# Cross-attention on one core: each square's first key block in two column parts

## The chip, the cores and the metric

The kernel runs on one core of a Trainium2 chip. The metric is the device time of one execution in microseconds, lower is better; for the kernel before it is the median of three runs.

## What is computed

Two batches of 2048 tokens with 640 channels attend, in 20 heads of 32 channels, to 77 text tokens and to 77 image tokens. Both have a softmax of their own, and the two results are added before the output projection.

```python
q = _split_heads(hidden_states @ Wq.T, H)
k = _split_heads(text @ Wk.T, H)
v = _split_heads(text @ Wv.T, H)
out_text = _merge_heads(_attend(q, k, v, sm_scale))
k_ip = _split_heads(ip @ Wk_ip.T, H)
v_ip = _split_heads(ip @ Wv_ip.T, H)
out_ip = _merge_heads(_attend(q, k_ip, v_ip, sm_scale))
out = out_text + IP_SCALE * out_ip
out = out @ Wo.T + bo
return out + residual
```

Everything is float32.

## The kernel before

The channels are cut in `NC` = 5 chunks of 128, that is four heads (`G` = 4) of 32 channels. A pair `q` is one chunk of one batch; there are 10 pairs. A unit `u` is half a pair's tokens (1024); there are 20. For each unit the kernel makes the queries (`queries`, line 201, in full 128x128 matmuls of 512 columns), the scores of each token against the 154 keys (`scores`, line 233), and the two softmaxes in the tensor `pb`, with the maximum, the exponential, the sum and the division shared among the vector, scalar and GpSimd engines (DVE, ACT, POOL). A 32x32 transpose on DVE (`transpose`, line 323) then turns the probabilities so that the keys lie on the partitions. The 154 keys fill `NK` = 5 blocks of 32 (the last has 26 and is filled up with zeros).

When both units of a pair are transposed, `attend` (line 332) multiplies with the values. The tensor engine is used as 16 tiles of 32x32, called squares here and numbered in the order of the code: row group `r` is the tile's rows and its PSUM bank (`pa[r]`), column group `g` the head and the 32 partitions of that bank. A matmul of one square and one key block `k` has 512 columns: 16 runs of 32 tokens each, in the layout that the transpose leaves. The loop goes block by block over all 16 squares, so a square's five blocks are accumulated in its own quarter of a bank. `v4s[q % 2]` holds the values, spread over the row groups by DMAs; `take_attention` (lines 355 and 359, on ACT) copies the four banks out, the first bank first.

The order of all work is written out by hand: each word of `SCHEDULE` emits one step on its engines. `A.q` is an attend, `CA.q` its copies out, `R` are scores, `q` queries, `m` and `F` the products of the output projection (lines 490, 500 and 848), `o` its last chunk (line 471), `k` and `v` the projections of keys and values (line 142). The 8 PSUM banks are two halves of four; the number behind an `@` names the half or the bank. The ten attends stand between queries or scores ahead of them and scores, queries or products behind them.

A float32 matmul is shown in the profile as two passes, each with its weight load: the 800 matmuls of line 332 are 1600 passes and 1600 loads.

Of the kernel before, what the change touches and what calls it, by code (L numbers as in the profile page):

```python
# [15 lines left out]
H, D, TEXT = 20, 32, 77  # L16
# [4 lines left out]
def kernel(  # L21
# [25 lines left out]
    nc = tc.nc  # L47
# [3 lines left out]
    G = P // D  # L51
# [9 lines left out]
    NK = (2 * L + D - 1) // D  # L61
# [28 lines left out]
    v4s = [const.tile([P, G, NK, D], F32, name=f"v4_{n}") for n in range(2)]  # L90
# [234 lines left out]
    def attend(q, pa):  # L325

        zones = pb[:, ds(q % 2, SUB)].rearrange("p z n g (k s) -> p (z n) g k s", k=NK)
        for k in range(NK):
            for r in range(G):
                rows = slice(r * D, (r + 1) * D)  # L330
                for g in range(G):
                    nc.tensor.matmul(  # L332
                        pa[r][g * D : (g + 1) * D, :],
                        v4s[q % 2][rows, g, k, :],
                        zones[rows, :, g, k, :],
                        start=(k == 0),
                        stop=(k == NK - 1),
                    )

    def rows_of_attention(b, c):  # L340

# [290 lines left out]
    def emit(word):  # L632
# [7 lines left out]
        elif k == "A":  # L640
            at[name] = halves[int(where)]
            attend(x, at[name])
        elif k == "CA":
            take_attention(x, at[f"A.{x}"])
# [246 lines left out]
```

## Time and profile before

| | |
|---|---|
| median of the runs | 497.76 us (497.68 to 497.79, 3 runs) |
| span of the profiled execution | 496.7 us |
| around the span, against the median | 1.06 us |
| TensorE busy with matmuls | 490.3 us (99%), 4114 passes |
| DVE, ACT, POOL busy | 408.5, 315.0, 362.5 us |
| line 332, the attends | 55.2 us in 10 pieces, 1600 passes |
| granted TensorE clock | full, in all 40 slices |

The profile is of one execution and gives its span, from the first to the last instruction; that execution's whole time isn't given apart from it, so the table sets the span beside the median. PE is the tensor engine's matmuls, PEld its weight loads. The listed durations of passes that follow one another overlap, so a busy PE isn't one at its peak. The chain that ended last is followed back from the last instruction, at each step to what released it.

### The profile page before, as it was taken

The page shows a single profiled execution, that of the slowest core. Times are in us where ns is not written, and L with a number is a line of the kernel's source. Part 1 is how long each engine was busy: PE and PEld are TensorE (multiplying, and loading weights), DVE is VectorE, ACT ScalarE, POOL GpSimd, SP SyncE. Part 2 cuts the span into 40 slices and gives each one's busy share as a digit, 9 for nine tenths or more (in the row PEclk, how much of TensorE's full clock was granted, in tenths as well). Part 3 has the DMA queues.
Part 4 walks back from the last instruction along what each step waited for, and adds up shares of the span by engine and source line. Part 5 has one row for each costly group of instructions (what it writes and reads, how often), then busy time and mean ns, then how long its engine had stood idle before and what let it go on. Part 6 is the DMA issues. An engine that isn't in the chain of part 4 may idle for free.

```text
span 496.7 us, 10482 instructions
## 1 busy us (share of the span) xinstructions
PE 490.3 (99%) x4114; PEld 287.9 (58%) x4114; DVE 408.5 (82%) x412; ACT 315.0 (63%) x1021; POOL 362.5 (73%) x157
## 2 busy tenths in 40 slices
PE   8999999999999999999999999999999999999997
PEld 5676657657547556456647654755755675444442
DVE  0069989979979989969976896687999978898877
ACT  1165878978978778668999786587578966100000
POOL 0069978798888999989874858565899888284830
PEclk9999999999999999999999999999999999999999
DMA  8991440332360454886445177418525401420115
GB/s 259 356 246 40 132 120 1 106 93 69 92 213 3 132 178 132 274 273 237 158 152 191 58 244 210 133 57 246 174 69 171 127 23 43 149 84 1 43 73 223
DMA packets 67474, 69.38 MB, mean 140 GB/s; under 512 B 5473, under 2 KB 47201, under 8 KB 67425
## 3 DMA queue, kind: packets, MB, share of 16 engines
q1 hardware_dynamic: 66704, 68.00, 43.8%
q8 instruction: 32, 0.52, 0.5%
q10 hardware_dynamic: 720, 0.72, 0.4%
q14 instruction: 18, 0.14, 0.1%
HBM read 54.94 MB, written 10.49 MB: 132 GB/s over the span
## 4 chain that ended last, share of the span: by engine, by line
PE 92%; DMA 3%; SPq 1%; DVE 1%; POOL 1%; ACT 1%; issue 0%; POOLq 0%
PE bank L201 33%; PE bank L848 11%; PE bank L490 10%; PE bank L233 10%; PE bank L332 10%; PE bank L142 9%; PE bank L471 6%; PE bank L500 3%; DMA aT<-in_L_xattn_Wk_ip_dram 2%; DMA wq<-in_L_xattn_Wq_dram 2%; SPq L534 1%; POOL pb L316 1%; DVE den L306 0%; ACT pb L301 0%; SPq L132 0%
## 5 line engine op out<-in xcount | busy, mean ns | idle before, releaser
L316 POOL TENSOR_TENSOR pb<-pb,rden 128x1848 f32<-128x1848 f32 (+1 forms) x60 | 176.1, 2944 | 39.7 <-DVE rden L311 35.5
L201 PE MATMUL bank<-x,wq 128*128 128x512 f32 x400 | 180.4, 601 | 0.6 <-DMA x<-in_x_dram 0.5
L295 POOL TENSOR_TENSOR pb<-pb,mx 128x1848 f32<-128x1848 f32 (+1 forms) x38 | 119.3, 3152 | 51.8 <-DVE mx L281 51.5
L201 PEld LDWEIGHTS bank<-x,wq 128*128 128x128 f32 x400 | 74.1, 191 | 86.7 <-issue 80.8
L323 DVE STREAM_TRANSPOSE pb<-pb 128x1920 f32<-128x1920 f32 (+1 forms) x60 | 115.7, 1932 | 4.9 <-POOL pb L316 4.3
L281 DVE TENSOR_REDUCE mx<-pb 128x24 f32<-128x1848 f32 (+1 forms) x51 | 93.7, 1850 | 30.7 <-ACT pb L245 30.5
L245 ACT COPY pb<-bank 128x462 f32<-128x462 f32 (+1 forms) x204 | 87.2, 539 | 36.0 <-PE bank L233 35.4
L306 DVE TENSOR_REDUCE den<-pb 128x24 f32<-128x1848 f32 (+1 forms) x47 | 88.7, 1895 | 17.6 <-ACT pb L301 13.3
L301 ACT ACTIVATE pb<-pb 128x1848 f32<-128x1848 f32 (+1 forms) x38 | 64.2, 1696 | 17.8 <-POOL pb L295 17.5
L269 ACT ACTIVATE pb<-pb,mx 128x77 f32<-128x77 f32 x224 | 67.8, 364 | 0.3 <-DVE mx L281 0.2
L233 PEld LDWEIGHTS bank<-kT,qT 32*128 32x128 f32 x1280 | 45.4, 184 | 26.9 <-issue 15.6
L269 ACT ACTIVATE pb<-bank,mx 128x77 f32<-128x77 f32 x184 | 51.8, 386 | 9.3 <-DVE mx L284 9.3
L233 PE MATMUL bank<-kT,qT 32*128 32x154 f32 x1280 | 56.2, 305 | 0.3 <-ACT kT L559 0.3
L332 PE MATMUL bank<-pb,v 32*32 32x512 f32 x1600 | 55.2, 597 | 0.0
L142 PE MATMUL bank<-wo_ct,aT 128*128 128x154 f32 x320 | 45.6, 296 | 0.3 <-DMA aT<-in_L_xattn_Wk_ip_dram 0.3
L142 PEld LDWEIGHTS bank<-wo_ct,aT 128*128 128x128 f32 x320 | 42.9, 188 | 3.6 <-issue 2.2
L332 PEld LDWEIGHTS bank<-pb,v 32*32 32x32 f32 x1600 | 29.9, 103 | 22.8 <-issue 10.7
L211 ACT ACTIVATE qT<-bank 128x512 f32<-128x512 f32 x40 | 24.2, 619 | 22.1 <-PE bank L201 22.0
L471 PE MATMUL bank<-aT,wo_ct 128*128 128x512 f32 x80 | 36.1, 596 | 0.0
L269 ACT ACTIVATION_READ_ACCUMULATOR pb<-bank,mx 128x1 f32 x128 | 33.6, 267 | 0.0
L490 PE MATMUL bank<-aT,wo_ct 128*128 128x256 f32 x128 | 32.3, 385 | 0.0
L490 PEld LDWEIGHTS bank<-aT,wo_ct 128*128 128x128 f32 x128 | 23.7, 190 | 6.5 <-issue 3.0
(75 smaller groups left out, 434.4 us busy)
## 6 DMA issues: line engine op xcount, KB each, us to landing
x<-in_x_dram SPq DMA_DIRECT2D x20, 1280.0 KB, 6.7
out_dram<-acc SPq DMA_DIRECT2D x20, 256.0 KB, 2.3
x<-in_x_dram SPq DMA_DIRECT2D x18, 256.0 KB, 5.9
acc<-in_x_dram SPq DMA_DIRECT2D x16, 256.0 KB, 4.7
out_dram<-x SPq DMA_DIRECT2D x15, 256.0 KB, 2.0
v<-vS SPq DMA_DIRECT2D x160, 20.0 KB, 2.8
wq<-in_L_xattn_Wq_dram SPq DMA_DIRECT2D x9, 320.0 KB, 5.0
aT<-in_L_xattn_Wk_dram SPq DMA_DIRECT2D x5, 512.0 KB, 5.5
```

Of the source, the lines that this page charges most:

```text
L142: nc.tensor.matmul(keys_in(out), loaded[n][:, k, :], cT[:, k, :, t, :], start=(k == 0), stop=(k == NCC - 1))
L201: nc.tensor.matmul(pq, wqs[q % 3][:, k, :], xs[place_of(u, h)][:, k, :], start=(k == 0), stop=(k == NC - 1),)
L233: nc.tensor.matmul(ps[g][:, ts(t, 2 * L)], qTs[(u, h)][g * D : (g + 1) * D, ts(st, P)], kT[g * D : (g + 1) * D, c, b].rearrange("p t l -> ...
L245: nc.scalar.copy(keys_of(u, s)[:, :, g], ps[g][:, : n * 2 * L].rearrange("p (n l) -> p n l", n=n))
L269: nc.scalar.activation(row, row if ps is None else rows_in(ps[g], n)[:, t, x], AF.Exp, bias=maxs[(u, s)][:, *one], accum_out=None if den i ...
L281: nc.vector.tensor_reduce(mx, rows_of(u, s), AX.X, ALU.max, negate=negate)
L295: nc.gpsimd.tensor_tensor(rows_of(u, s), rows_of(u, s), maxs[(u, s)].unsqueeze(3).to_broadcast([P, n, 2, L]), ALU.subtract)
L306: nc.vector.tensor_reduce(den_of(u, s), rows_of(u, s), AX.X, ALU.add)
L316: nc.gpsimd.tensor_tensor(rows_of(u, s), rows_of(u, s), rdens[(u, s)].unsqueeze(3).to_broadcast([P, n, 2, L]), ALU.mult)
L323: nc.vector.transpose(p, p)
L332: nc.tensor.matmul(pa[r][g * D : (g + 1) * D, :], v4s[q % 2][rows, g, k, :], zones[rows, :, g, k, :], start=(k == 0), stop=(k == NK - 1),)
L490: nc.tensor.matmul(part, w_of[m][:, kp, op], t_of(m, b, i)[:, kp], start=(op == kp == 0 and m in (1, 2, 5)), stop=(op == 1 and kp == 1 and ...
```

## The change

`attend` alone is changed. For key block 0, the 32 columns of each of the 16 runs are cut in two: square `i` (0 to 15) first does the first `12 + i` of 32, which starts the accumulation. Then the blocks 1 to 4 follow whole, over all squares in the same order. At the end, square `i` does the remaining `20 - i` columns of block 0, and that matmul ends the accumulation. An attend has 96 matmuls in place of 80; the products computed are the same ones.

```diff
-        for k in range(NK):
-            for r in range(G):
-                rows = slice(r * D, (r + 1) * D)
-                for g in range(G):
-                    nc.tensor.matmul(
-                        pa[r][g * D : (g + 1) * D, :],
-                        v4s[q % 2][rows, g, k, :],
-                        zones[rows, :, g, k, :],
-                        start=(k == 0),
-                        stop=(k == NK - 1),
-                    )
+        squares_of = [(r, g) for r in range(G) for g in range(G)]
+        FIRST_PART, STEP = 12, 1
+
+        def part(k, i, lo, hi, start, stop):
+            r, g = squares_of[i]
+            rows = slice(r * D, (r + 1) * D)
+            nc.tensor.matmul(
+                pa[r][g * D : (g + 1) * D, :].rearrange("p (n s) -> p n s", s=D)[:, :, lo:hi],
+                v4s[q % 2][rows, g, k, :],
+                zones[rows, :, g, k, lo:hi],
+                start=start,
+                stop=stop,
+                skip_group_check=True,
+            )
+
+        for i in range(G * G):
+            part(0, i, 0, FIRST_PART + STEP * i, True, False)
+        for k in range(1, NK):
+            for i in range(G * G):
+                part(k, i, 0, D, False, False)
+        for i in range(G * G):
+            part(0, i, FIRST_PART + STEP * i, D, False, True)
```

## The prediction

> **What bounds the kernel now.** I read the profile page first, then the chain of waits, then the one line that the change touches, in slices down to 10 ns. A change of 0.2% is 1.0 us here, about what a measurement of this kernel can tell from none.
>
> From the page of the kernel before: busy time by engine, and the shares of the chain that ended last.
>
> ```profile
> span 496.7 us, 10482 instructions
> PE 490.3 (99%) x4114; PEld 287.9 (58%) x4114; DVE 408.5 (82%) x412; ACT 315.0 (63%) x1021; POOL 362.5 (73%) x157
> PE 92%; DMA 3%; SPq 1%; DVE 1%; POOL 1%; ACT 1%; issue 0%; POOLq 0%
> ```
>
> TensorE carries the chain, so what the change does to TensorE's own time reaches the end nearly whole. Two attends from that chain in order of time, and a plain full-array stretch of ten passes beside them:
>
> ```profile
> 36.01 4.29 PE bank L201 x10
> 69.85 5.45 PE bank L332 x153
> 106.94 5.45 PE bank L332 x154
> ```
>
> Ten passes of 512 columns with nothing in between take 4.29 us. An attend also gives each 32x32 tile of the array ten passes of 512 columns (five key blocks, each matmul shown as two passes), all 16 tiles side by side, and it takes 5.45 us. The difference, 1.16 us an attend and 11.6 us in all ten, is time in which tiles wait although TensorE is called busy. Where it goes is seen in the summary of line 332 (and of line 233, for a second length) and in slices of the first attend, of line 332's instructions alone; the columns are busy us and, in brackets, the instructions at work in the slice, for matmul passes (PE) and for weight loads (PEld).
>
> ```profile
> L332 PE MATMUL bank<-pb,v x1600: 584/587/612, 69.8 to 428.6; 32*32 32x512 f32 x178
> L233 PE MATMUL bank<-kT,qT x1280: 289/289/394, 24.4 to 403.9; 32*128 32x154 f32 x183
> 69.77:69.83 0.06, 0.05 (x8) 0.05 (x12) 1.00 1.21 290
> 69.83:69.90 0.07, 0.07 (x8) 0.07 (x17) 1.00 1.31 300
> 69.90:69.93 0.03, 0.03 (x12) 0.03 (x17) 1.00 1.28 307
> 70.04:70.07 0.03, 0.03 (x16) 0.03 (x8) 1.00 1.46 341
> 70.81:70.82 0.01, 0.01 (x17) 0.00 (x0) 1.00 0.87 205
> 70.82:70.83 0.01, 0.01 (x16) 0.00 (x0) 1.00 2.09 512
> 70.84:70.85 0.01, 0.01 (x13) 0.00 (x1) 1.00 0.84 205
> 70.84:71.30 0.46, 0.46 (x29) 0.42 (x31) 1.00 0.58 136
> 71.30:71.91 0.61, 0.61 (x33) 0.24 (x3) 1.00 0.06 15
> 71.91:72.37 0.46, 0.46 (x31) 0.41 (x29) 1.00 0.16 36
> 72.37:72.98 0.61, 0.61 (x34) 0.37 (x5) 1.00 0.00 0
> ```
>
> Two durations give the length of any pass: 512 columns 587 ns, 154 columns 289 ns, so 0.83 ns a column (427 ns for 512) and 160 ns until the end is seen. Weight loads come in bursts (31 in 0.46 us, then 3 in 0.61 us): a block's loads are held back and then go together. The first load of each of the four later bursts, from the timeline of the loads in slices of 15 ns:
>
> ```profile
> 70.85 0.10 PEld L332 LDWEIGHTS bank<-pb,v 32*32 32x32 f32 x1
> 71.92 0.10 PEld L332 LDWEIGHTS bank<-pb,v 32*32 32x32 f32 x1
> 73.00 0.10 PEld L332 LDWEIGHTS bank<-pb,v 32*32 32x32 f32 x1
> 74.07 0.10 PEld L332 LDWEIGHTS bank<-pb,v 32*32 32x32 f32 x1
> ```
>
> The period is 1.073 us, not the 0.854 that two passes need. What lets a burst go is in the 10-ns slices. Tile 0 starts at 69.78; its second pass starts 0.45 later (70.23) and ends 0.587 after that, at 70.82, where the count falls from 17 to 16. About 0.03 us later the first load appears, although tile 0 already had its next pass. I read it so: the load of tile s+1 for the next block may go only when tile s has ended both passes of this block. The two stand 65 instructions apart (16 tiles, each with two loads and two passes). One link is then 0.587 (second pass to its end) + 0.036 (to the next tile's first pass) + 0.450 (that pass, with weights not loaded ahead: 0.427 + 0.023) = 1.073, the period seen. Each link goes one block and one tile on. The lost time is 0.219 a block; streaming doesn't set it.
>
> **The change, part by part.** It touches this line alone. Engines DVE, ACT, POOL and SP keep their instructions in their order; on PE every attend gets 16 more matmuls. The start of the first attend (bank 71 is row group 0, bank 72 row group 1), before and then after:
>
> ```order
> L332 MATMUL bank_71<-pb,v_0_80 32x512 [waits DMAHW0_49,DVE_49,Activation_49]
> L332 MATMUL bank_71<-pb,v_0_80 32x512 [waits DMAHW4_49]
> L332 MATMUL bank_71<-pb,v_0_80 32x512 [waits DMAHW6_49]
> L332 MATMUL bank_71<-pb,v_0_80 32x512 [waits DMAHW2_49]
> L332 MATMUL bank_72<-pb,v_0_80 32x512 [waits DMAHW1_49,Activation_49]
> ```
> ```order
> L334 MATMUL bank_71<-pb,v_0_80 32x16x12 [waits DMAHW0_49,DVE_49,Activation_49]
> L334 MATMUL bank_71<-pb,v_0_80 32x16x13 [waits DMAHW4_49]
> L334 MATMUL bank_71<-pb,v_0_80 32x16x14 [waits DMAHW6_49]
> L334 MATMUL bank_71<-pb,v_0_80 32x16x15 [waits DMAHW2_49]
> L334 MATMUL bank_72<-pb,v_0_80 32x16x16 [waits DMAHW1_49,Activation_49]
> ```
>
> The waits stay on the same tiles; only the width differs, from 12 of 32 columns in tile 0 to 27 in tile 15. The end of the same attend, before and after, with the scores that follow:
>
> ```order
> L332 MATMUL bank_73<-pb,v_0_80 32x512 x4
> L332 MATMUL bank_74<-pb,v_0_80 32x512 x4
> L233 MATMUL bank_67<-kT,qT_0_408 128x154 [waits Activation_49]
> L233 MATMUL bank_68<-kT,qT_0_408 128x154 [waits Activation_49]
> L233 MATMUL bank_69<-kT,qT_0_408 128x154
> ```
> ```order
> L334 MATMUL bank_74<-pb,v_0_80 32x16x8
> L334 MATMUL bank_74<-pb,v_0_80 32x16x7
> L334 MATMUL bank_74<-pb,v_0_80 32x16x6
> L334 MATMUL bank_74<-pb,v_0_80 32x16x5
> L233 MATMUL bank_67<-kT,qT_0_408 128x154 [waits Activation_49]
> ```
>
> Sixteen short matmuls now stand between the last whole block and the next line's work.
>
> *What it takes away.* Streaming per tile is the same (the two parts make one block), but tile 0 ends its first part early, and starts are spread: by 2 x 16 x 0.83 = 27 ns more from tile to tile. The first release comes sooner. *What it adds.* One more link at the end, because the last part is a sixth round. I sum along the chain that ends last, in us from the attend's start. It ends in tile 15's last part. Each link moves one tile on, so five links lead back to tile 10's first part:
> - tile 10 starts at 0.14 (third group of starts, in the slice 69.90:69.93). Its 22 of 32 columns are 352 a pass: 0.294. Second pass at 0.14 + 0.294 + 0.023 = 0.457, end at 0.457 + 0.294 + 0.160 = 0.911;
> - tile 11, block 1: 0.911 + 0.036 = 0.947, second pass at 0.947 + 0.450 = 1.397;
> - three full links of 1.073 (tiles 12, 13, 14): second pass of tile 14, block 4, at 4.616, end at 5.203;
> - tile 15's last part, 5 of 32 columns, 80 a pass (0.067): 5.203 + 0.036 = 5.239, second pass at 5.329, streamed at 5.396.
>
> What follows an attend now is in the timeline of the first one and the next, and of ACT's copies out of the banks:
>
> ```profile
> 69.78 5.52 PE L332 MATMUL bank<-pb,v 32*32 32x512 f32 x160
> 75.23 0.54 PE L233 MATMUL bank<-kT,qT 32*128 32x154 f32 x8
> 106.88 5.52 PE L332 MATMUL bank<-pb,v 32*32 32x512 f32 x160
> 112.03 2.31 ACT L359 COPY aT<-bank 128x256 f32<-128x256 f32 x8 [0.30 <-PE bank L332]
> ```
>
> Before, the last pass starts at 5.52 - 0.587 = 4.93, is streamed at 5.36, and the next line starts at 75.23 - 69.78 = 5.45, which is 0.09 behind. After: 5.396 + 0.09 = 5.49. So an attend gets 0.04 us longer, and ten of them 0.4 us. The same links for before: the last burst starts at 74.07 - 69.78 = 4.29; the tiles behind it follow at the rate of the burst (31 loads in 0.46, two loads a tile, under 0.03 us each); the last pass starts 0.64 behind the burst's first load. The trace holds that directly, so only the after side is derived.
>
> *Bounds of the unknown.* No row shows a pass of short runs (12 to 27 columns out of each 32). The nearest are the 128x154 and 32x512 passes, which agree on a fixed 160 ns, so I take length by columns. If a pass of short runs cost nothing extra the figure above stands; if both parts cost as much as a full block, an attend gains a link of 1.073. Below zero: tile 10's start at 0.14 holds 0.08 us of delay that the tiles from 8 on have now (8 passes at work in 69.83:69.90, 12 only from 69.90). Each of those groups begins with a matmul that waits for more than one semaphore; if the delay were gone, the chain would begin at 0.06 and an attend would end 0.04 us earlier than now.
>
> *Instruction count.* The 16 matmuls are 32 passes and 32 loads. In 69.77:69.83 eight passes start in 0.06 us, 7.5 ns each; 32 of these are 0.24 us an attend if none of it hides. I take nothing, since they go out while other tiles stream. The Trainium skill, TensorEngine Tiling (Array Packing), section Performance Considerations, says the opposite of such splits: each matmul carries about 60 cycles of overhead, so short ones gain nothing from being short. With TensorE: Matmul & The Clock Gate (its section on the back-to-back gap gives about 25 ns for those cycles), 32 passes would be an estimated 0.8 us an attend and the time 505.8; the eight starts in 0.06 us speak against it as a serial cost.
>
> **The rivals.**
> - *Slower, later banks.* If a bank's last pass counts as ended only in program order, bank 0 (tiles 0 to 3) is free for ACT when tile 15's block 4 has ended: its second pass, one tile behind tile 14's at about 33 ns, starts at 4.65 and ends at 5.24. Today the copies start at 112.03 - 106.88 = 5.15, some 0.03 after their bank ends at 5.12. That is 0.12 us later for the copies, and ACT, DVE and POOL behind them. If TensorE waits for it, 0.16 an attend: +1.6, 499.4 us. It decides as soon as any work behind the copies has less than 0.12 us to spare. Against it: TensorE has other banks to fill after each attend, and ACT's wait there is 0.30.
> - *Slower, short passes pay.* With the 7.5 ns of each start in full: 0.28 an attend, +2.8, 500.6 us; short runs at a full block's price: +10.7, 508.5 us. For it stands only that no row has such a pass.
> - *Faster, no link at the end.* If the last part of tile 15 didn't wait for tile 14 but followed its own block 4, it would start at 4.65 + 0.427 = 5.08, its second pass at 5.15, and be streamed at 5.21; next line at 5.30: 0.15 less an attend, -1.5, 496.3 us. It needs a release two instructions earlier than the one I read at 70.82 to 70.85. The Trainium skill, TensorE: Matmul & The Clock Gate, its specification table, gives the queue 64 entries with a partial reorder window; by that rule, which the slices bear out as 65 instructions between an end and the load it releases, the link stays and the time is 498.2.
> - *Faster, the spread breaks the bursts.* If bursts collide for another reason than the link, tiles spread by 33 ns would run free: 4.29 + 0.27 of starts + 0.09 of streams to fill a sixth round, about 4.7 an attend, -7.5, 490.3 us. Against it: the first load of each burst lies 1.073 apart four times running, as the link says.
> - *The delay ahead of tile 8 goes away:* -0.4, 497.4 us, within 0.2%.
>
> **How the numbers follow.** The profiled execution's span is 496.7 us, the median of the runs 497.76; the 1.06 around the span I leave as it is. 497.76 + 0.4 = 498.2 us. Chances: my forecast 0.52, the delay gone 0.06, both within 0.2%: 0.58. Later banks 0.20 and short passes that pay 0.08, slower: 0.28. No link at the end 0.09, free tiles 0.05, faster: 0.14. The range 497.0 to 499.4 takes in the forecast, the lost delay and the later banks; left out are paying passes, free tiles and the missing link, about 0.22.
>
> **What would show it.** In the changed kernel an attend should hold 192 passes and last 5.56 us (5.52 now), the next line should start 5.49 behind it, the first load of later bursts should still lie 1.07 apart, and the last second pass should start at 5.33. ACT's copies should start about 5.27 behind the attend's start where ACT waits for them. An attend under 5.4 us makes the link wrong; over 5.7, the price of a short pass. Equal attends with another total would put the cause behind the banks, on ACT or POOL.

## The result and the profile after

The changed kernel takes 501.12 us (median of 13 runs), against 497.76 before: ratio 1.007, 95% interval 1.0051 to 1.0088. It is slower, and outside the range of 497.0 to 499.4. It also scatters: 13 runs of before beside it lie between 497.14 and 499.5, those of the changed kernel between 497.21 and 504.0. Two of them (497.21, 498.11) are as fast as before, six lie from 499.9 to 501.3, five from 503.1 to 504.0. Those five have a mean granted TensorE clock of 0.993; the others 0.997 to 1.

The profiled execution is one of the five: 503.11 us, span 501.3. (So some 1.8 us lie around a span, not the 1.06 that I had from one profile and a median of other runs. It moves no step.) From its page, the span, the busy times and the shares of the chain:

```profile
span 501.3 us, 11122 instructions
PE 493.9 (99%) x4434; PEld 304.0 (61%) x4434; DVE 408.7 (82%) x412; ACT 315.0 (63%) x1021; POOL 362.5 (72%) x157
PE 98%; issue 1%; DVE 0%; ACT 0%
```

Nothing but TensorE's own work and "issue" is on the chain: time in which TensorE waited for nothing that the profile shows. The waits of TensorE name the place:

```profile
PE bank L334 <- issue: 2.1, 1, 2.1
```

One wait of 2.1 us, inside an attend. From the timeline of TensorE in the changed kernel: the second attend, the third, and the seventh in two pieces with the line behind it and the eighth.

```profile
105.67 5.57 PE L334 MATMUL bank<-pb,v 32*32 32x192 f32 x192
142.81 5.50 PE L334 MATMUL bank<-pb,v 32*32 32x192 f32 x192
299.91 3.83 PE L334 MATMUL bank<-pb,v 32*32 32x192 f32 x111
305.82 3.95 PE L334 MATMUL bank<-pb,v 32*32 32x512 f32 x81 [2.09 <-issue]
309.70 6.36 PE L482 MATMUL bank<-aT,wo_ct 128*128 128x512 f32 x10
350.80 5.57 PE L334 MATMUL bank<-pb,v 32*32 32x192 f32 x192
```

The same places before:

```profile
301.17 5.52 PE L332 MATMUL bank<-pb,v 32*32 32x512 f32 x160
306.62 4.56 PE L471 MATMUL bank<-aT,wo_ct 128*128 128x512 f32 x10
346.21 5.52 PE L332 MATMUL bank<-pb,v 32*32 32x512 f32 x160
```

The second and third attends are as forecast (5.56). The seventh stops after 111 passes for 2.09 us, and then everything is slow: ten passes take 6.36 us in place of 4.56. From the seventh to the eighth attend it is now 350.80 - 299.91 = 50.89 us, before 346.21 - 301.17 = 45.04: 5.85 us are lost here. (The two spans differ by 4.6 only, since in this execution the first attend, and with it the seventh, began 1.26 us earlier than in the profile of before: 68.52 against 69.78, ahead of any changed instruction.) Slices of that stretch, with all engines; the last three columns are granted clock, DMA share and GB/s:

```profile
301.00:302.00 1.00, 1.00 (x51) 0.76 (x36) 0.00 (x0) 1.00 (x1) 1.00 (x1) 1.00 0.93 342
302.00:303.00 1.00, 1.00 (x41) 0.65 (x21) 0.72 (x1) 0.25 (x1) 1.00 (x1) 1.00 1.07 416
303.00:304.00 1.00, 0.74 (x14) 0.00 (x0) 1.00 (x1) 0.00 (x0) 0.62 (x1) 1.00 0.76 281
304.00:305.00 1.00, 0.00 (x0) 0.00 (x0) 0.97 (x3) 0.00 (x0) 0.16 (x1) 1.00 0.04 6
306.50:313.50 7.00, 7.00 (x77) 3.23 (x54) 3.17 (x4) 2.56 (x5) 6.54 (x5) 0.51 0.87 276
```

Until 303 the DMA engines are full. Then TensorE has nothing, not even loads, and after the stop its clock is halved: 0.51 in the mean of 7 us. In the trace's clock record the half lasts 6.83 us, which costs an estimated 3.4. 2.09 of stop and 3.4 of clock leave some 0.3 of the 5.85; I put that down to running dry and filling again, which isn't shown apart.

What TensorE waited for is in the table of DMA queues. For the whole kernel, the queue that brings TensorE's instructions, before and after; then its packets in the stretch from 297.3 to 303.4 (there is only the data queue, q1) and from 303.4 to 304.45:

```profile
q8 instruction: 32, 0.52, 0.5%
```
```profile
q8 instruction: 35, 0.57, 0.5%
```
```profile
q1 hardware_dynamic: 799, 1.48, 76.4%
```
```profile
q1 hardware_dynamic: 68, 0.11, 28.2%
q8 instruction: 1, 0.02, 6.2%
```

A packet is 16 KB. 4434 passes and 4434 loads are 8868 instructions, 34.6 times 256; before, 8228, 32.1 times. So each packet is a block of 256 TensorE instructions (the run e2 below, with 256 more than before, has one packet more). By the count of TensorE's instructions in the trace, a border between blocks lies 30 instructions into the seventh attend (158 in the kernel before); the block behind it was fetched from 303.41 to 304.44, when the x load of 1280 KB was through, and TensorE stopped 193 instructions past the border. It went on at 305.82, 1.4 us after the block had landed. Two things this count can't tell. The trace shows when a block's transfer began, not when it was asked for. And the zero of the count isn't fixed, since TensorE may have had instructions ahead of the first that is listed: eight stops in seven of the traces here come at the same place, 193 past a border counted so, and that shows the spacing of 256, while the block may as well end just where TensorE stops.

### The profile page after: what moved, and what is told of

Same layout as the page of the kernel before. It is cut to its first block, busy times and chain, and to the rows that moved or that the text cites. A ratio compares the mean times of both kernels' runs of the same rounds, so it can differ in the third digit from the quotient of the medians.

```text
span 501.3 us, 11122 instructions
## 1 busy us (share of the span) xinstructions
PE 493.9 (99%) x4434; PEld 304.0 (61%) x4434; DVE 408.7 (82%) x412; ACT 315.0 (63%) x1021; POOL 362.5 (72%) x157
## 4 chain that ended last, share of the span: by engine, by line
PE 98%; issue 1%; DVE 0%; ACT 0%
PE bank L201 35%; PE bank L859 11%; PE bank L334 11%; PE bank L233 10%; PE bank L501 10%; PE bank L142 9%; PE bank L482 7%; PE bank L511 3%; PE bank L560 1%; DVE acc L805 0%; ACT pb L245 0%; ACT kT L570 0%; DVE pb L558 0%
## 5 line engine op out<-in xcount | busy, mean ns | idle before, releaser
L334 PE MATMUL bank<-pb,v 32*32 32x512 f32 (+15 forms) x1920 | 57.5, 536 | 2.1 <-issue 2.1
L334 PEld LDWEIGHTS bank<-pb,v 32*32 32x32 f32 x1920 | 45.3, 103 | 18.6 <-issue 7.7
L482 PE MATMUL bank<-aT,wo_ct 128*128 128x512 f32 x80 | 37.9, 621 | 0.0
```

The source lines that it names most:

```text
L334: nc.tensor.matmul(pa[r][g * D : (g + 1) * D, :].rearrange("p (n s) -> p n s", s=D)[:, :, lo:hi], v4s[q % 2][rows, g, k, :], zones[rows, : ...
```

## The experiments

The theory to test (the fetch theory): the attend itself costs nothing, but 64 more instructions in each attend move the block borders and use up blocks faster; in the seventh attend a block is asked for while a 1280 KB load holds the DMA engines, comes late, and TensorE runs dry. The rivals: the cost is inside the changed attends (links, short passes), or the clock falls on its own because short passes are less activity. The four runs e1 to e4 share their runs of before (497.55 us, 15 runs), e5 to e8 theirs (497.64, 31), and e9 and e10 theirs (497.86, 15).

**The load taken away (e3).** In the changed kernel's order the x load goes behind the attend.

```diff
-S1.14 LX.17.1 SS.1.4 I0.14 cm1.1 A.6@1 ... SF.1.3 cq.15.1 LX.17.0
+S1.14 SS.1.4 I0.14 cm1.1 A.6@1 ... SF.1.3 cq.15.1 LX.17.1 LX.17.0
```

> The changed kernel with one 1280 KB load of x (unit 17, second half) moved in SP's order from ahead of the 7th attend to behind it, right before the unit's other load. The instruction block that came late then has no such transfer ahead of it. Fetch theory: no idle time of TensorE in the 7th attend, no half clock, attends of 5.49 to 5.57 us, 497.5 to 498.3, and the scatter falls to under 1 us. Rival (short passes lower the activity and the clock falls): still slow, 500 to 504, scattered. Rival (the attend's own cost): 500 to 501.

Measured: 497.94 us (497.5 to 498.56, 11 runs), ratio 1.0006 (0.9997 to 1.0015). No idle "issue" time, and the seventh attend whole; the timeline, and the DMA queues from 299 to 301, where the block now comes in time:

```profile
300.13 5.50 PE L334 MATMUL bank<-pb,v 32*32 32x192 f32 x192
```
```profile
q8 instruction: 1, 0.02, 4.0%
```

All ten attends are in two parts, and the loss and the scatter are gone. Both rivals fall: the mean clock is 0.998 to 1 in all 11 runs, and the attends cost next to nothing (0.03 us in all ten, worked out below).

**The borders moved, no attend changed (e1).** Behind the warm-up of the kernel before:

```diff
+    for n in range(32):
+        r, g = divmod(n % (G * G), G)
+        rows = slice(r * D, (r + 1) * D)
+        nc.tensor.matmul(
+            banks[r][g * D : (g + 1) * D, :D], warm[rows, :D], warm[rows, :D], start=True, stop=True
+        )
```

> The kernel before, attends as they were, with 32 tiny 32x32 matmuls (32 columns) added behind the warm-up, in TensorE's first idle time: 128 more instructions (64 passes, 64 loads) ahead of everything. They move the borders of the 16 KB blocks (256 instructions) in which TensorE's instructions arrive; in the 7th attend a border comes 30 instructions in, as in the changed kernel, in place of 158. Fetch theory: TensorE runs dry in the 7th attend for about 1.5 to 2.5 us (and perhaps in the 5th, whose border also moves, 79 in), with a stretch of half clock behind it in some executions: 499.5 to 505 us, scattered by several us. Rival (the cost is inside the changed attend: links, short passes): no stall, 497.8 within 0.5.

Measured: 502.2, 502.35, 506.14 and 506.57 us, ratio 1.0132 (1.0095 to 1.0169); the two long ones, over the 505 expected, at a mean clock of 0.993, as in the changed kernel. The timeline of the fifth and the seventh attend, each in two pieces:

```profile
211.50 5.12 PE L332 MATMUL bank<-pb,v 32*32 32x512 f32 x136
217.51 1.12 PE L332 MATMUL bank<-pb,v 32*32 32x512 f32 x24 [0.89 <-issue]
302.71 4.31 PE L332 MATMUL bank<-pb,v 32*32 32x512 f32 x111
308.63 2.22 PE L332 MATMUL bank<-pb,v 32*32 32x512 f32 x49 [1.61 <-issue]
```

The seventh stops after 111 passes, the very count of the changed kernel, with the same border. The kernel before has the fault in it; where its borders lay, it was hidden. The fifth attend has another transfer beside it: a weight load of 1600 KB was issued at 206.47, and the DMA engines are full from 209 to 217 us (a share of 1.02 or more in each 1-us slice).

**A whole block more (e2).** The same with `range(64)`, 256 instructions, so that the borders are back in place.

> The same with 64 tiny matmuls, 256 instructions, one whole block: the borders fall where they fell in the kernel before. Fetch theory: no stall over 0.5 us, 497.8 within 0.7 (the extra matmuls lie in idle time). Rival (added early matmuls cost by themselves): more than the kernel with 32 of them.

Measured: 500.02 us (499.77 to 501.37), ratio 1.0051 (1.0037 to 1.0065), over the expectation. But the loss is at the front: the first attend starts late, at 71.07 us, against 69.31 in the kernel with only the load moved (e8, below) and at most 69.9 in any other trace. Two things show there. The 128 tiny passes take 1.54 us that weren't hidden. And the 512-column passes behind them start 0.85 us apart until 10.2 us and 0.43 after that, while e8 makes the same change at 7.0: the clock record has the full clock only from 10.3 us, where the others have it from 4.2 to 6.9. How much each costs, and whether the tiny passes bring the second about, wasn't tested. Behind the front all ten attends are 5.52 to 5.54 us, with no stop. So it is the borders that make e1's stops, while 64 early matmuls have a price that I had put at nothing. The tiny passes, the first attend and the seventh of this run, then the first attend of e8:

```profile
4.34 1.54 PE L553 MATMUL bank<-pb 32*32 32x32 f32 x128
71.07 5.52 PE L332 MATMUL bank<-pb,v 32*32 32x512 f32 x160
302.46 5.52 PE L332 MATMUL bank<-pb,v 32*32 32x512 f32 x160
```
```profile
69.31 5.52 PE L332 MATMUL bank<-pb,v 32*32 32x512 f32 x160
```

**Only the seventh (e5), and all but the seventh (e6).** In `attend`, ahead of the parts, with `q != 6` or `q == 6`:

```diff
+        if q != 6:
+            for k in range(NK):
+                for i in range(G * G):
+                    part(k, i, 0, D, k == 0, k == NK - 1)
+            return
```

> Only the 7th attend in two parts, the other nine as before. The instruction border lies 158 in, where the kernel before has it; only the rate at which instructions are used rises (384 in 5.5 us in place of 320). Fetch theory: TensorE reaches the end of what it holds about 194 past the border, 352 in, at 5.0 us; the late block is usable near 6.4: a stall of 0 to 1.5 us, 498 to 501.5. If the border's place is all that counts, 497.6 within 0.5. If parts slow an attend by themselves, 497.6 and an attend over 5.6.

Measured: 499.10 us (498.51 to 499.62, 8 runs), ratio 1.0028 (1.0018 to 1.0038).

> All attends in two parts but the 7th, which is whole as before. The border lies 30 in, as in the changed kernel, and the attend uses 320 instructions. Fetch theory: a stall of about 2 us in an attend that isn't changed, 499.5 to 504.5, as for the changed kernel. Rival (cost inside the changed attends): under the changed kernel's time by a tenth of its loss only, with no stall in the 7th.

Measured: 500.17 us (497.65 to 503.38, 10 runs), ratio 1.0054 (1.003 to 1.0078). The seventh attend of each, of the first with parts and of the second without:

```profile
300.04 5.44 PE L334 MATMUL bank<-pb,v 32*32 32x192 f32 x175
306.62 0.51 PE L334 MATMUL bank<-pb,v 32*32 32x208 f32 x17 [1.14 <-issue]
```
```profile
301.46 4.32 PE L334 MATMUL bank<-pb,v 32*32 32x512 f32 x111
307.68 2.22 PE L334 MATMUL bank<-pb,v 32*32 32x512 f32 x49 [1.91 <-issue]
```

One attend in parts is enough for a stop (the rate, with the border where it was), and nine of them make the tenth, unchanged one stop (the border). Both halves of the theory hold. The medians are 1.5 and 2.5 us over before, but they don't measure the two halves: two of e6's runs (503.28 and 503.38) have a mean clock of 0.993, two (497.65 and 497.69) are as fast as before, and in e5's trace the ninth attend, not changed, is long too (6.06 us, 5.54 in the kernel before; not followed).

**The two stops of e1 apart (e10).** The kernel before with 32 tiny matmuls and the load moved.

> The kernel before with 32 tiny matmuls and the x load moved behind the 7th attend. Of the two stalls that the 32 matmuls brought, the one in the 7th attend has lost the transfer ahead of it and the one in the 5th has not. Fetch theory: 7th attend 5.52, 5th about 7.1 us; 499.0 to 501. Rival (the shift slows all attends near a border, whatever the transfers): both stalls stay, 502 to 506.

Measured: 500.16 us (499.79 to 501.67, 4 runs), ratio 1.0044 (1.0028 to 1.0059).

```profile
210.87 5.12 PE L332 MATMUL bank<-pb,v 32*32 32x512 f32 x136
217.44 1.12 PE L332 MATMUL bank<-pb,v 32*32 32x512 f32 x24 [1.45 <-issue]
304.33 5.52 PE L332 MATMUL bank<-pb,v 32*32 32x512 f32 x160
```

The fifth attend, whose transfers stayed, still stops; the seventh, whose load is gone, doesn't. So the stop of the seventh took both, a border in the wrong place and a transfer beside it.

**The links by themselves (e4).** `FIRST_PART, STEP = 12, 0`.

> The changed kernel with STEP = 0: every square's first part is 12 of 32 columns, the last part 20; the instructions and their number are the same. Tells the sum by links: the last part then is 320 columns a pass for tile 15, and the first part gives no spread. The chain from the attend's start: tile 10's first part ends at 0.14 + 0.160 + 0.023 + 0.160 + 0.160 = 0.64, tile 11's second pass 1.13, three links 4.35, end 4.93, tile 15's last part 4.97, second pass 5.26, but the slower links through the loads at 17 ns a tile make it about 5.5 streamed: the attend's listed length 5.70 (5.49 to 5.57 with STEP = 1). If short passes have a fixed price and no links, 5.55. The stall in the 7th attend is expected here as well, since the instruction counts are those of the changed kernel.

Measured (one run): 502.63 us, with a stop of 1.90 us in the seventh attend. The second and the fifth:

```profile
106.26 5.72 PE L334 MATMUL bank<-pb,v 32*32 32x192 f32 x192
211.56 5.72 PE L334 MATMUL bank<-pb,v 32*32 32x192 f32 x192
```

5.70 was expected, and 5.55 without links: the sum by links holds. (All ten have this length but for the seventh's stop.)

**What the links allow (e7).** If the links are right, a steeper start helps: 6, 8, ... 30 columns, the last three squares whole and so without a sixth round.

```diff
-        FIRST_PART, STEP = 12, 1
+        FIRST_PART, STEP = 6, 2
...
+        cut = [min(D, FIRST_PART + STEP * i) for i in range(G * G)]
```

> FIRST_PART 6, STEP 2, and squares whose first part would be the whole block (13 to 15) not cut; the x load moved behind the 7th attend as before. By the links, worked tile by tile: the steeper first parts let every tile's release come earlier than the tile needs it in the first blocks, and the last tiles have no sixth round. Listed attend 5.33 us without the delay at tile 8 and 5.39 with it, against 5.52: 0.13 to 0.19 less in each, 1.6 us in all: 496.0 within 0.5 where no block of instructions comes late. Rival (the attend's length is set by the number of matmuls, 93 against 96): 5.46 to 5.54 and no gain.

Measured: 498.15 us (497.54 to 498.29, 11 runs), ratio 1.0008 (0.9999 to 1.0016): no gain. The kernel before with the same load moved (e8) is the control:

> The kernel before with the same x load moved. It has no stall to lose in the 7th attend in most executions: 497.6 within 0.4, the same as the kernel before. If the move by itself gains or costs, it shows here, and the version with STEP 2 is to be read against this one.

Measured: 497.71 us (497.3 to 498.28, 11 runs), ratio 1.0001 (0.9992 to 1.001). So moving the load neither gains nor costs. In e7 the attends were short as expected (the seventh 5.34), but the third and the tenth were longer. In the third TensorE again ran dry 193 instructions past a border, for 0.66 us from pass to pass; the tenth lost its time in smaller pieces. Their 0.88 and 0.39 us over 5.34 are more than half of the 2.1 us that e7 missed its expectation by; the rest I didn't follow.

```profile
143.22 6.22 PE L334 MATMUL bank<-pb,v 32*32 32x96 f32 x186
300.73 5.34 PE L334 MATMUL bank<-pb,v 32*32 32x96 f32 x186
423.11 5.73 PE L334 MATMUL bank<-pb,v 32*32 32x96 f32 x186
```

So I moved the borders with 14 tiny matmuls behind the warm-up (e9).

> The version with STEP 2 and the later load, with 14 tiny matmuls (56 instructions) behind the warm-up. In the version without them the 3rd and the 10th attend ran dry (listed 6.22 and 5.73 us in place of 5.34), with borders 46 and 32 instructions in; the shift puts these borders ahead of the attends, where instructions are used slowly. Fetch theory: all ten attends 5.33 to 5.40, 496.3 to 497.3, faster than the kernel before. Rival (the STEP 2 attend stalls on its own account): the 3rd and 10th as long as they were, 498.1.

Measured: 497.16 us (496.55 to 498.09, 11 runs), ratio 0.9988 (0.9979 to 0.9997).

```profile
143.62 5.34 PE L334 MATMUL bank<-pb,v 32*32 32x96 f32 x186
300.23 5.34 PE L334 MATMUL bank<-pb,v 32*32 32x96 f32 x186
422.62 5.34 PE L334 MATMUL bank<-pb,v 32*32 32x96 f32 x186
```

Both long attends are gone, with the borders alone moved. In the medians this version is 0.7 us under before, an interval that just leaves out no gain, and far under the changed kernel. Nine attends gave 0.14 to 0.18 us each, the second (listed 5.47, not followed) 0.05: about 1.6 us. Where the other 0.9 went was not followed either; one candidate, in the waits of TensorE of this execution and untested, is the start:

```profile
PE bank L201 <- DMA x<-in_x_dram: 0.8, 1, 0.8
```

## Why the prediction was wrong

**The attend: right, and a little too dear.** The link of 1.073 us, the sixth round's link and the switch of 0.09 held: 5.57 listed where I had 5.56, 5.72 and 5.34 in the variants where the links gave 5.70 and 5.33. The release 65 instructions back is the reading that these sums rest on; no run tried it alone. One term was mis-sized: I put the 0.08 us of delay ahead of tile 8 into all ten attends. I had looked at the first; by the trace's starts only four of the ten have it. Those end at 5.57, the other six at 5.49 to 5.50. Added over e3, the next lines start 54.55 us behind their attends in place of 54.51: 0.03 for all ten, where I had 0.4.

**The step that failed: "Instruction count".** I priced 32 passes and 32 loads by what they take on the engine, found them covered by other tiles' streaming, and took nothing. That cover is real. The step that failed is taking the engine for the whole price: I left out that instructions have to be fetched. In its place the runs showed a stop of 2.09 us in one attend, with 6.83 us of half clock behind it in the profiled execution, and 501.12 us in the median; with one load moved away from that block's transfer the same attends give 497.94. The changed attend uses 384 instructions in 5.5 us, a block of 256 in 3.7, while a full-array line uses two in 0.43. The rows to see it stood in the page of before: queue q8 with its 32 packets, and the DMA share. Even the near miss was there: in the kernel before that queue's packet came at 305.23 to 306.24, at the end of the seventh attend (301.17 to 306.69).

**The rivals.** *Later banks* was right that the copies come later, and its price was wrong. ACT's copies in the second and third attends, and in the third before:

```profile
111.01 2.31 ACT L370 COPY aT<-bank 128x256 f32<-128x256 f32 x8 [0.48 <-PE bank L334]
148.08 2.05 ACT L366 COPY aT<-bank 128x512 f32<-128x512 f32 x4 [0.52 <-PE bank L334]
```
```profile
149.12 2.05 ACT L355 COPY aT<-bank 128x512 f32<-128x512 f32 x4 [0.41 <-PE bank L332]
```

They start 111.01 - 105.67 = 5.34 and 148.08 - 142.81 = 5.27 behind the attend. Before it is 5.15 in both (149.12 - 143.97 in the third), so they come 0.19 and 0.12 later; the forecast was 0.12, for an attend like the second. The time didn't pay for it: e3 is level with before. *Short passes pay* and *free tiles* fell with the same run and with e4, and *no link at the end* with the 5.57. The 505.8 of 0.8 us an attend didn't come either, with e3's 0.03 us for all ten. *The delay ahead of tile 8 goes away* didn't happen: the four attends that have it before have it still. The sign I gave the larger part of the odds outside 0.2% (slower, 0.28) was the right one, but for none of the reasons given, and the range had no term for a stall that comes in some executions and not in others.

**The fetch, row and rule.** The Trainium skill, Runtime: NRT & Kernel Launch, section Instruction fetch mechanics, has the block of 16 KiB and 256 instructions and calls the crossing of a border mostly hidden, without a branch at least. The blocks agree with this trace (35 packets of 16 KB for 8868 instructions). The hiding fails for one of them, in straight-line code: 2.09 us of stop, because the block's own transfer came only when 1280 KB of data were through.

The half clock is less settled. It follows the stop in the profiled execution of the changed kernel, and a mean clock of 0.993 marks all of its runs over 503 us, e1's over 506 and e6's over 503. Slices behind the stops of 1.91 us in e6 and of 1.45 us in e10 (granted clock is the third number from the end):

```profile
307.70:314.00 6.30, 6.30 (x59) 2.58 (x58) 3.52 (x4) 2.55 (x5) 6.30 (x5) 1.00 0.74 217
```
```profile
219.00:222.20 3.20, 3.20 (x6) 1.20 (x5) 1.06 (x2) 3.12 (x5) 3.20 (x2) 0.54 0.36 70
```

The longer stop kept the full clock and the shorter one lost it for 3 us. So the length of the stop doesn't decide it alone; what does was not tested.

## What to carry to other kernels

Where small matmuls follow one another fast (here 59 to 70 instructions per us, against 5 in full-array lines), count instructions as a transfer too: find the instruction queue's packets, where the borders fall, and which large load is under way there. If a kernel's time begins to scatter after an edit that only adds instructions, look for "issue" waits in the middle of a line, and try moving a load away or shifting the borders by a few early instructions before judging the edit itself. A chain of releases read at 10 ns could be summed by hand here and held; but check in how many places each of its terms occurs.

## What the hardware showed that I hadn't expected

- A TensorE instruction block, once its transfer began, took about 1.0 us, and TensorE went on 1.2 to 1.4 us after it had landed (the stops of the seventh attend in the changed kernel, e1, e4, e5 and e6).
- All eight stops (the changed kernel, e1 and e10's fifth attends, the seventh in e1, e4, e5 and e6, the third in e7) came at the same place in the count of 256, and 463 to 495 instructions after the last block had landed: under two blocks.
- After a stop of 2.09 us the clock was half for 6.83 us, so the stop cost more than twice its length; the stops of 1.90 and 1.91 us in e4 and e6 left the clock full.
- Steeper first parts took 0.18 us off an attend (5.34 against 5.52) although they add 13 matmuls to it: in these attends the spread of the starts counted for more than the number of matmuls.
